# Row sums of the second attention's exponentials: VectorE or GpSimd

## The chip, the cores and the metric

The kernel runs on one core of a Trainium2 chip. The metric is the device time of one execution in microseconds (us), and the median of several runs is compared. A core has five engines with queues of their own: TensorE (PE, with its weight loads shown as PEld), VectorE (DVE), ScalarE (ACT), GpSimd (POOL) and SyncE (SP), which issues most transfers. Each engine takes its instructions in the order of its queue and waits for the others by semaphores. SBUF is the working memory with 128 partitions; PSUM has eight banks of 128x512 f32, into which TensorE writes.

## The reference

One decoder layer on 8 sequences of 100 tokens of width 1024, with a context of 722 tokens for each sequence:

```
x = layernorm(x + retention_attention(x))           # first attention, 8 heads
x = layernorm(x + attention(x, context))            # second attention
x = layernorm(x + (silu(x Wg) * (x Wu)) Wd)         # feed-forward, 4096 hidden
```

The second attention has 16 query heads of 128 that share 4 key/value heads. Its keys are the 722 context tokens followed by the 100 own tokens (causal among themselves):

```
scores = q . k_full * scale + mask       # 100 x 822 for a head
probs  = softmax(scores)                 # exp(scores - max) / sum of exp
out    = (probs . v_full) wo
```

Everything is computed to f32 accuracy.

## The kernel before

All matrix products are made from halves: a value is split into a rounded high part and a low part (`split` and `split2`, line 68: ScalarE casts the high part, VectorE subtracts it from the value to get the low part), and `mm3` (lines 90, 93 and 94) issues three matmuls for each product.

The second attention loops over the 8 sequences `b` and, in each, over the 4 key/value heads `kv`: 32 steps, called heads below. A head holds the 4 query heads that share its keys, so that a row of scores has 4 x 100 = 400 columns, and the 822 keys lie on the partitions, in seven blocks of up to 128. They are worked in the order 6, 5, 0, 1, 2, 3, 4 (`ORDER`); block 6 is small, 54 keys by 216 columns. One head does this:

- `context_keys` and `context_values` project the context (split into the `big` tiles, once for each sequence, by `load_context`) into keys and values. The squares of the keys are summed over the partitions by a GpSimd all-reduce (L706, tile `kss`); the sums go out as a row and come back as a column (L710 and L801), and lines 803 to 810 make the factors `rk` from them. A small GpSimd memset (L700) sets the tail of `kss` after the earlier row has left.
- For each block, TensorE makes the scores in a PSUM bank `s` (4 banks); ScalarE (L830) or VectorE (L826, with the mask) puts them into block `j` of the tile `s` in SBUF, and VectorE keeps the running maximum `mx` (L831, L834). GpSimd's all-reduce over the partitions (L141) gives the maximum `mb` of each column.
- In four steps of 1, 2, 2 and 2 blocks, VectorE subtracts the maximum (L841, L845), ScalarE takes the exponential (L847) and casts the high part `ph`, VectorE makes the low part `pl` (both L68), and VectorE adds the blocks into `sm` (L850; L853 for the small block).
- A second GpSimd all-reduce (L141) adds `sm` over the partitions into `sb`. TensorE multiplies the exponentials with the values into the only PSUM bank `v`.
- Lines 864 to 869 take the reciprocal of `sb` and scale the product; the result is split (`oh`) and sent out (L872).

The tile `s` in SBUF has one buffer: the next head's first scores may be written only when the exponentials of this one have been read. The key tiles `kall` have two. A planner in the compiler's front end sets the order of the instructions on every engine from its own cost estimates and the program's order (`schedule_with_timeline_sim=True`), so that the work of neighbouring heads is interleaved. In the last heads the output projection of the first half of the tokens (`out_proj`) fills TensorE.

Of the kernel before, what the change touches and what calls it, by code (L numbers as in the profile page):

```python
# [11 lines left out]
ALU = mybir.AluOpType  # L12
# [15 lines left out]
R6 = SC + T - 6 * P  # L28
T6 = T - R6
N6 = 4 * R6  # L30
# [10 lines left out]
def decoder_layer(ctx, tc, xT, cT, w1, wo1, w2, wo2, wc, w3, wd, gw, qw, kw, trig, dec, mask, out):  # L41
    nc = tc.nc
# [17 lines left out]
    def bt(ap):  # L60
        return ap.rearrange("p (b t) -> p b t", b=NB)
# [5 lines left out]
    def split2(hi, lo, src):  # L67
        return nc.scalar.copy(hi, src), nc.vector.tensor_tensor(lo, src, f32(hi), ALU.subtract)  # L68
# [70 lines left out]
    def all_red(pool, x, tag, op=RED.add):  # L139
        y = pool.tile([P, N], F32, tag=tag, name=tag)  # L140
        nc.gpsimd.partition_all_reduce(y, x, P, op)  # L141
        return y
# [623 lines left out]
    with sbuf("cx", 2) as p, sbuf("c1", 1) as p1:  # L766

        s = p1.tile([P, NC, N], F32, tag="s", name="s")
# [5 lines left out]
        for b in range(B):  # L774
            if b > 0:
                load_context(b)
            for kv in range(NKV):
# [34 lines left out]
                if b + kv > 0:  # L812
                    s = p1.tile([P, NC, N], F32, tag="s", name="s")
                mx = p.tile([P, N], F32, tag="mx", name="mx")
                def part(ap, c):
                    ap = bt(ap)
                    return ap[0:R6, :, T6:] if c == 6 else ap
# [19 lines left out]
                sm = p.tile([P, N], F32, tag="mx", name="sm")  # L837
                for j0, j1 in ((0, 1), (1, 3), (3, 5), (5, 7)):
                    if j0 == 0:
                        e = s[0:R6, 0, :N6]  # L840
                        nc.vector.tensor_tensor(bt(e), bt(e), part(mb, 6), ALU.subtract)  # L841
                        hl = ph[0:R6, 0, :N6], pl[0:R6, 0, :N6]
                    else:
                        e = s[:, j0:j1]
                        nc.vector.tensor_tensor(e, e, mb[:, None, :].to_broadcast([P, j1 - j0, N]), ALU.subtract)  # L845
                        hl = ph[:, j0:j1], pl[:, j0:j1]
                    nc.scalar.activation(e, e, AF.Exp)  # L847
                    split2(*hl, e)
                    for j in range(max(j0, 2), j1):
                        nc.vector.tensor_tensor(sm, s[:, 1] if j == 2 else sm, s[:, j], ALU.add)  # L850
                    if j0 == 1:
                        s6 = part(sm, 6)
                        nc.vector.tensor_tensor(s6, s6, bt(s[0:R6, 0, :N6]), ALU.add)  # L853
                sb = all_red(p, sm, "mb")
                ov = bank("v")[:, :N]
                for j in (1, 0, 2, 3, 4, 5, 6):
# [413 lines left out]
```

## Time and profile before

| what | value |
|---|---|
| median of 3 runs | 2486.41 us (2483.72 to 2486.9) |
| span of the profiled execution | 2480.1 us; its own total is not given beside the span |
| second attention in the span | 830 to 1610 us |
| busy there: PE, DVE, ACT, POOL | 776.0, 705.3, 469.8, 298.8 us of 780 |
| granted TensorE clock | 1.00 there, 0.999 over the span |
| mean of an addition, L850 and L853 | 0.63 and 0.37 us, on DVE |
| all-reduce of the maxima, of the sums | 1.60 and 2.60 us, on POOL |

The profile is that of one execution. Its span runs from the first to the last instruction; the time of a run holds what lies around the span as well. A group of instructions is listed by line, engine, operation and tiles, then the count, the busy time, the mean of one in nanoseconds, and the time its engine was idle just before, with what ended that idle time. A wait `A <- B` tells that A's engine stood idle until B was done. Windows give each engine's busy time in a stretch of the span. A line with `x2` or `x3` in the timeline merges neighbours of the same kind. `L68` is the helper for all splits, so its groups are told apart by their tiles.

### The profile page before, as it was taken

How to read it: one execution, taken by the hardware profiler on the slowest of the kernel's cores; microseconds unless marked ns; L12 is line 12 of the kernel's file. 1: busy time of each engine (PE TensorE's matmuls, PEld its weight loads, DVE VectorE, ACT ScalarE, POOL GpSimd, SP SyncE). 2: the span in 40 equal slices, each digit the busy share in tenths (PEclk: the TensorE clock that was granted, in tenths of full speed). 3: DMA queues.
4: the chain of work that ended last, by engine and by line, in shares of the span. 5: the costliest groups of instructions: out<-in, count | busy, mean ns of one | idle time of the engine just before them, and what ended most of it. 6: DMA issues, size and time to landing. Idle time of an engine off the chain costs nothing.

```text
span 2480.1 us, 37239 instructions
## 1 busy us (share of the span) xinstructions
PE 2456.9 (99%) x14068; PEld 2436.3 (98%) x14068; DVE 1950.7 (79%) x3101; ACT 1341.0 (54%) x2258; POOL 481.8 (19%) x266
## 2 busy tenths in 40 slices
PE   9999999999999999999999999999999999999997
PEld 9999999999999999999999999999999999999997
DVE  7777877556898798998998999757987777666756
ACT  6667676334888565665566666524544454432221
POOL 0111111100566343443443443100000000000000
PEclk9999999999999999999999999999999999999999
DMA  7333345775544555455455454465455444389731
GB/s 244 112 112 129 132 142 186 242 257 182 173 163 144 196 185 175 130 180 165 154 181 156 155 187 170 156 241 172 160 176 189 161 161 161 122 303 325 265 103 54
DMA packets 221891, 433.98 MB, mean 175 GB/s; under 512 B 47338, under 2 KB 163946, under 8 KB 209294
## 3 DMA queue, kind: packets, MB, share of 16 engines
q1 hardware_dynamic: 217358, 419.49, 50.2%
q0 software_dynamic: 3200, 10.75, 1.9%
q8 instruction: 111, 1.82, 0.3%
q10 hardware_dynamic: 1152, 1.34, 0.2%
q14 instruction: 70, 0.57, 0.1%
HBM read 322.18 MB, written 109.35 MB: 174 GB/s over the span
## 4 chain that ended last, share of the span: by engine, by line
PE 94%; DVE 2%; DMA 2%; ACT 1%; issue 1%; SPq 0%; DVEq 0%; ACTq 0%
PE a L94 20%; PE a L93 20%; PE a L90 20%; PE s L94 9%; PE s L93 9%; PE s L90 9%; PE v L93 2%; PE v L94 2%; PE v L90 2%; PE s L554 1%; PE s L795 1%; PE s L166 1%; DVE y L331 0%; PE v L546 0%; DMA wst<-in_w 0%
## 5 line engine op out<-in xcount | busy, mean ns | idle before, releaser
L90 PE MATMUL a<-big,w 128*128 128x400 f32 (+2 forms) x1808 | 610.7, 339 | 2.0 <-DVE z L270 0.7
L93 PE MATMUL a<-big,w 128*128 128x400 f32 (+2 forms) x1808 | 610.0, 337 | 0.5 <-DVE big L68 0.5
L94 PE MATMUL a<-big,w 128*128 128x400 f32 (+2 forms) x1808 | 608.5, 337 | 0.5 <-DVE w L68 0.5
L68 ACT CAST w<-wst 128x1024 fp32r<-128x1024 f32 (+1 forms) x231 | 239.5, 1039 | 380.3 <-PE s L94 147.6
L68 DVE TENSOR_TENSOR w<-wst,w 128x1024 fp32r<-128x1024 f32 (+1 forms) x231 | 281.1, 1217 | 132.5 <-ACT w L68 130.6
L90 PEld LDWEIGHTS a<-big,w 128*128 128x128 f32 x1808 | 340.2, 188 | 4.5 <-ACT big L68 1.1
L93 PEld LDWEIGHTS a<-big,w 128*128 128x128 f32 x1808 | 340.9, 189 | 2.5 <-DVE big L68 1.3
L94 PEld LDWEIGHTS a<-big,w 128*128 128x128 f32 x1808 | 340.8, 189 | 1.4 <-DVE w L68 0.8
L90 PE MATMUL a<-z,w 128*128 128x400 f32 x680 | 235.0, 346 | 0.4 <-ACT w L68 0.4
L93 PE MATMUL a<-z,w 128*128 128x400 f32 x680 | 235.1, 346 | 0.0
L94 PE MATMUL a<-z,w 128*128 128x400 f32 x680 | 234.9, 346 | 0.0
L90 PE MATMUL s<-big,w 128*128 128x400 f32 x664 | 230.3, 347 | 0.5 <-DMA big<-o2d 0.4
L94 PE MATMUL s<-big,w 128*128 128x400 f32 x664 | 229.2, 346 | 0.4 <-DVE w L68 0.4
L93 PE MATMUL s<-big,w 128*128 128x400 f32 x664 | 229.5, 346 | 0.0
L706 POOL PARTITION_ALL_REDUCE kss<-ksq x64 | 170.2, 2659 | 113.4 <-ACT ksq L705 112.6
L141 POOL PARTITION_ALL_REDUCE ss<-sq x56 | 148.4, 2651 | 199.3 <-ACT sq L750 110.1
L830 ACT ACTIVATE s<-s,rk 128x400 f32<-128x400 f32 x160 | 88.1, 591 | 90.9 <-DVE sm L850 65.3
L90 PEld LDWEIGHTS a<-z,w 128*128 128x128 f32 x680 | 127.8, 188 | 1.2 <-ACT w L68 0.8
L94 PEld LDWEIGHTS a<-z,w 128*128 128x128 f32 x680 | 128.7, 189 | 0.0
L93 PEld LDWEIGHTS a<-z,w 128*128 128x128 f32 x680 | 127.8, 188 | 0.4
L90 PEld LDWEIGHTS s<-big,w 128*128 128x128 f32 x664 | 124.8, 188 | 2.1 <-issue 0.7
L94 PEld LDWEIGHTS s<-big,w 128*128 128x128 f32 x664 | 125.4, 189 | 0.7 <-DVE w L68 0.7
(366 smaller groups left out, 5462.3 us busy)
## 6 DMA issues: line engine op xcount, KB each, us to landing
wst<-in_w SPq DMA_DIRECT2D x135, 512.0 KB
w<-wcd SPq DMA_DIRECT2D x64, 1024.0 KB
wst<-in_wo SPq DMA_DIRECT2D x64, 512.0 KB
hd<-h SPq DMA_DIRECT2D x12, 1400.0 KB
wst<-in_wd SPq DMA_DIRECT2D x64, 256.0 KB
big<-o1d SPq DMA_DIRECT2D x16, 800.0 KB
qd<-d SPq DMA_DIRECT2D x32, 400.0 KB
q<-qd SPq DMA_DIRECT2D x32, 400.0 KB
```

What stands on the lines that cost most here:

```text
L68: return nc.scalar.copy(hi, src), nc.vector.tensor_tensor(lo, src, f32(hi), ALU.subtract)
L90: i = nc.tensor.matmul(acc, lh, rh, start=start, stop=False, skip_group_check=chain)
L93: nc.tensor.matmul(acc, lh, rl, start=False, stop=False, skip_group_check=chain)
L94: nc.tensor.matmul(acc, ll, rh, start=False, stop=stop, skip_group_check=chain)
L141: nc.gpsimd.partition_all_reduce(y, x, P, op)
L166: nc.tensor.transpose(tr[0:T, b * P:(b + 1) * P], vt[:, b * T:(b + 1) * T], ident)
L554: nc.tensor.matmul(bt(o)[:, b], vv[:, b * P:(b + 1) * P], pf[:, b], start=True, stop=True)
L706: nc.gpsimd.partition_all_reduce(ss[:, at], sq[:, at], P, RED.add)
L795: nc.tensor.transpose(tr[0:rows, (c - c0) * P:(c - c0 + 1) * P], vt[:, c * P:c * P + rows], ident)
L830: nc.scalar.activation(sc, sp, AF.Copy, scale=rk[:, c:c + 1])
```

## The change

The additions of lines 850 and 853 are issued on GpSimd instead of VectorE. Tiles, order in the program, and all other instructions stay as they are.

```
                     for j in range(max(j0, 2), j1):
-                        nc.vector.tensor_tensor(sm, s[:, 1] if j == 2 else sm, s[:, j], ALU.add)
+                        nc.gpsimd.tensor_tensor(sm, s[:, 1] if j == 2 else sm, s[:, j], ALU.add)
                     if j0 == 1:
                         s6 = part(sm, 6)
-                        nc.vector.tensor_tensor(s6, s6, bt(s[0:R6, 0, :N6]), ALU.add)
+                        nc.gpsimd.tensor_tensor(s6, s6, bt(s[0:R6, 0, :N6]), ALU.add)
```

## The prediction

> **What bounds the kernel now.** I began with the page's busy table and its chain, to see which engine sets the end; then the busy time in stretches, with the second attention (830 to 1610 us) cut into 100 us pieces; then TensorE's own waits in it.
>
> ```profile
> PE 2456.9 (99%) x14068; PEld 2436.3 (98%) x14068; DVE 1950.7 (79%) x3101; ACT 1341.0 (54%) x2258; POOL 481.8 (19%) x266
> PE 94%; DVE 2%; DMA 2%; ACT 1%; issue 1%; SPq 0%; DVEq 0%; ACTq 0%
> ```
>
> ```profile
> 930.00:1030.00 100.00, 100.00 (x608) 99.36 (x607) 90.37 (x156) 60.11 (x117) 40.49 (x21) 1.00 0.49 156
> ...
> 1700.00:2000.00 300.00, 298.47 (x1629) 296.58 (x1628) 245.42 (x355) 151.03 (x223) 0.00 (x0) 1.00 0.46 161
> ```
>
> ```profile
> PE v L93 <- DVE pl L68: 1.8, 2, 1.6
> PE s L90 <- DVE vall L68: 1.5, 1, 1.5
> PE a L90 <- DVE z L270: 0.7, 1, 0.7
> ```
>
> In the stretches the columns after the length are PE, PEld, DVE, ACT, POOL, then granted clock and DMA. All six 100 us pieces from 930 to 1530 show PE at 100.00 and clock 1.00; 830 to 930 has 98.47, 1530 to 1610 (80 us) has 77.52. PE is therefore idle 1.53 + 2.48 = 4.0 us in the whole stage, and the waits add to the same 4.0. A busy PE could hide stalls inside its modelled ends, but its pace says no: in the feed-forward layer, 300 us hold 1,629 matmuls, 0.184 us each, nearly all 400 columns wide; the attention's 608 in 100 us (0.164 us each) mix 400 columns with 360, 216 and 128.
>
> VectorE is the second engine: the eight pieces sum to 705.3 us of 780. The all-reduces of the sums run from 853.16 to 1596.67 us, 31 periods, so a head takes 24.0 us; over 32 heads VectorE has 22.0 us busy and 2.3 us idle each. POOL has 298.8 us in the stage, 9.3 a head.
>
> **The change part by part.**
>
> ```profile
> L850 DVE TENSOR_TENSOR sm<-sm,s 128x400 f32<-128x400 f32 x128 | 80.8, 631 | 0.8
> L850 DVE TENSOR_TENSOR sm<-s 128x400 f32<-128x400 f32 x32 | 19.2, 600 | 0.0
> L853 DVE TENSOR_TENSOR sm<-sm,s 54x216 f32<-54x216 f32 x32 | 11.8, 368 | 0.0
> L141 POOL PARTITION_ALL_REDUCE mb<-mx x32 | 51.0, 1595 | 90.4 <-DVE mx L831 90.4
> L141 POOL PARTITION_ALL_REDUCE mb<-sm x32 | 83.3, 2602 | 208.9 <-DVE sm L850 208.9
> L700 POOL MEMSET kss<- 128x46 f32 x29 | 4.0, 137 | 63.8 <-DMA row<-kss 63.8
> L773 POOL MEMSET vall<- 128x256 f32 x2 | 0.6, 311 | 8.5 <-DMA kd<-d 8.5
> ```
>
> These groups of the stage show, after the bar, busy us, mean ns of one, and the idle time before.
>
> *Removed from VectorE:* 160 + 32 additions, 80.8 + 19.2 + 11.8 = 111.8 us, 3.5 us a head. Off the path, because PE does not wait for VectorE from 930 to 1530. Of the 4.0 us of PE idle, only the 1.8 us for the lows of the exponentials (`pl`), in the last heads, sit behind these additions; I credit 1.0.
>
> *Added to POOL:* five 128x400 additions and one 54x216. No POOL addition is in this trace. Bounds: VectorE's 0.56 us below, the adding all-reduce's 2.60 above. The two memsets give 174 ns for 210 more columns, 0.83 ns a column and pass, so 0.43 us for writing 400. An addition has two reads and a write: 0.76 us if a read runs beside the write, 1.1 if nothing overlaps. I take 1.0 us, nearest to the memsets, and 0.6 for the small one: 5.6 us a head. With VectorE's 0.56 and 0.37 it is 3.2, with the all-reduce's 2.60 (and 216/400 of it) 14.4. POOL then has 9.3 + 5.6 = 14.9 us of 24.0 (12.5 to 23.7), not a bound by amount.
>
> A rule speaks against the change. The Trainium skill, "GPSIMD Engine Reference", section 4.1 (Engine selection), wants elementwise work on VectorE and calls GpSimd about twice as slow; its table for 2048 columns has 4497 against 2293 ns. By it, an estimate from that page, an addition costs 1.96 x 0.56 = 1.1 us and a head about 6.2 us, without a single PE wait more, as POOL would have 15.5 of 24.0 us. No run here shows it yet.
>
> *The engines meet.* POOL's and VectorE's instructions hold each other up when both read pairs from SBUF. A head's two timelines show it:
>
> ```profile
> 1276.90 2.46 POOL L706 PARTITION_ALL_REDUCE kss<-ksq  x1
> 1285.43 3.07 POOL L706 PARTITION_ALL_REDUCE kss<-ksq  x1 [4.63 <-ACT ksq L705]
> 1289.39 2.60 POOL L141 PARTITION_ALL_REDUCE mb<-sm  x1 [0.89 <-DVE sm L850]
> ```
>
> ```profile
> 1277.03 1.74 DVE L841 TENSOR_TENSOR s<-s,mb 54x216 f32<-54x216 f32 x1 [0.33 <-POOL mb L141]
> 1286.12 2.57 DVE L850 TENSOR_TENSOR sm<-sm,s 128x400 f32<-128x400 f32 x2
> 1289.35 0.37 DVE L826 SCALAR_TENSOR_TENSOR s<-s,msk 54x216 f32<-54x216 f32 x1
> ```
>
> L841 took 1.74 us beside an all-reduce; its shortest is 0.36. Summing mean less undisturbed duration over the stage's VectorE groups (L841 16 us, L831 19, the `oh` split 11, L850 9, L834 7, the context splits 6, L866 5, L809 5) gives about 79 us, 2.5 a head, against 9.3 of POOL work: 27% of POOL's time is lost on VectorE. By that share the additions cost VectorE 5.6 x 0.27 = 1.5 us a head; if all of it collides, 5.6. They run while VectorE makes the lows from pairs in SBUF, so I take 60%, 3.4. Net of the 3.5 removed: -0.1 (between -2.0 and +2.1), below its 2.3 us of idle. Cost on PE nothing; if that cover went, each us past it would cost 32 us in all. The Trainium skill, "SBUF — State Buffer", section "Who interferes with whom", has the loser blocked for the whole instruction; L841's 1.74 us agrees in kind. Taken literally for every addition it is the 5.6 us case.
>
> *The new order.* The additions now stand in POOL's queue behind the memset of `kss`, which waits for a row transfer (63.8 us in 29 times), and ahead of or behind the next key norm's all-reduce (L706) and the sums' own (L141). Who waits: that all-reduce, then L864 to L872; the row transfer and the factors `rk`, if L706 stands behind; and, since the tile `s` has one buffer, the next head's first evictions (L826 on VectorE, L830 on ScalarE, with the key and value evictions queued behind). ScalarE already waits there: 65.3 us in 24 times for L850. In the head shown the last exponential ended at 1283.0 and the sum at 1289.3, 6.3 us later, as VectorE had the lows to make. POOL could begin near 1281.0 and needs 5.6, so 1286.6; if the key all-reduce goes first (2.5), 1289.1. Level, so nothing. In the head before, exponentials ended at 1255.7, the sum at 1263.3, and POOL stood idle from 1253.0 to 1263.3: there it is earlier. The later sum all-reduce has cover: its `v` bank is read (L869) at 1296.68 us while the next products into it come after the next exponentials, which start at 1299.41.
>
> Every DMA stays on its queue; POOL's own transfer issues in the stage are five, at its end (L264, after the last sum). SP issues nothing new. The planner reorders the engines' work by its own costs; I price that at 0, with 3 us to either side. Sum: -1.0 (removed) + 0 (additions on POOL) + 0 (meeting) + 0 (order) = -1.0. The profiled span is 2480.1 us, so 2479.1; the page gives no total for that execution beyond the span, and the median of the three runs lies 6.3 above it (3.6 to 6.8): 2485.4.
>
> **The rivals.**
>
> *The sum comes late (slower).* Place: L826 and L830 waiting on POOL. For: one buffer of `s`, and ScalarE's 65.3 us. Against: POOL's 6.5 us of idle before each sum all-reduce (208.9/32). Price: 1281.0 + 5.6 + 3.3 (POOL held by the four lows) + 2.5 (key all-reduce) = 1292.4, 3.1 later than 1289.3. Heads without context work take 22.0 us between their L841 (1277.03 to 1299.01), against 24.0 on average: 2.0 us of slack. It decides above that: 1.1 us x 32 = 35 us, 2521; in one head of four, 9 us, 2495.
>
> *VectorE becomes the bound (slower).* It decides when it loses more than 3.5 + 2.3 = 5.8 us a head, just past the 5.6 of full collision. With additions of 1.3 us (7.2 a head) and all colliding, 1.4 x 32 = 45 us, 2531; at 14.4 us a head, (14.4 - 5.8) x 32 = 275 us, 2761, which needs both far ends. Against: the measured share is 27%.
>
> *The freed VectorE clears PE's idle (faster).* At most all 4.0 us of the stage, 2482; that is under 0.2%, so a real gain needs the planner to shorten another stage too, where PE idles 3.0 us before 600 and 16.1 after 1610.
>
> **How the numbers follow.** About 0.2%, 5 us, is what a measurement of this kernel can tell from no change. Forecast 0.55 (own range 2481 to 2490); late sum 0.22; VectorE bound 0.17; a gain past 5 us 0.06. So faster 0.06, same 0.55, slower 0.39. The low end is the full clearing and 2 us of the order's 3, 2480; the high end 2518 reaches into both slow rivals and leaves some 0.14 above and 0.03 below.
>
> **What the changed profile would show.** Right: L850 and L853 on POOL near 1.0 and 0.6 us; VectorE near 705 us in the stage, POOL near 480; PE still at 100.00 per 100 us; the period of the sum all-reduces still 24.0. Late sum: ScalarE's wait L830 <- POOL `sm` well above 65 us, and PE waiting at `s` or `a`. VectorE bound: its busy share above 97%, `pl` and L845 lengthened, PE waiting for `pl`. I am wrong if the additions take much over 1.3 us, or if the planner's new order puts PE's score products where they wait for `s`.

## The result and the profile after

The changed kernel takes 2865.18 us in the median (2859.82 to 2868.61) against 2485.43 us (2483.72 to 2486.9): 1.1524 times as long, 95% interval 1.1508 to 1.154. The forecast was no change.

The page of the changed kernel: the busy table, rows of the 40 slices, and the chain by engine.

```profile
PE 2571.2 (90%) x14068; PEld 2524.6 (88%) x14068; DVE 1876.3 (65%) x2909; ACT 1329.3 (46%) x2258; POOL 690.9 (24%) x458
PE   9999999999996677777878877777999999999998
POOL 0001001016643344444444444442000000000000
PEclk9999999999997888888898898888999999999999
PE 57%; POOL 13%; issue 11%; DVE 8%; DMA 5%; ACT 5%; SPq 0%; POOLq 0%; DVEq 0%; ACTq 0%
```

TensorE is no longer busy all through the second attention; elsewhere it is as before. GpSimd and "issue" (time in which an engine waited for nothing that the profile shows) are now a quarter of the chain. In stretches, with the same columns as before:

```profile
930.00:1030.00 100.00, 69.33 (x380) 67.11 (x378) 45.15 (x76) 32.69 (x65) 39.39 (x27) 0.86 0.28 87
1330.00:1430.00 100.00, 76.74 (x408) 74.17 (x407) 56.47 (x94) 42.78 (x83) 44.40 (x32) 0.89 0.38 120
```

VectorE fell from 90 us in a hundred to 45 to 56, so it has not become the bound. Where the time is, the groups on GpSimd in the stage tell; the last columns are the idle time before them and what ended it:

```profile
L850 POOL TENSOR_TENSOR sm<-sm,s 128x400 f32<-128x400 f32 x128 | 133.3, 1041 | 23.0 <-issue 15.2
L141 POOL PARTITION_ALL_REDUCE mb<-sm x32 | 83.8, 2618 | 192.9 <-issue 192.9
L141 POOL PARTITION_ALL_REDUCE mb<-mx x32 | 51.7, 1615 | 92.1 <-DVE mx L831 92.1
L850 POOL TENSOR_TENSOR sm<-s 128x400 f32<-128x400 f32 x32 | 39.3, 1227 | 236.0 <-issue 73.5 <-ACT big L68 35.9 <-DVE rk L810 27.7
L853 POOL TENSOR_TENSOR sm<-sm,s 54x216 f32<-54x216 f32 x32 | 21.4, 668 | 2.5
```

The additions cost what was forecast (1.04 us, the first of each head 1.23, and 0.67 for the small one). But GpSimd stands idle 236.0 us ahead of the 32 first additions, 7.4 us each, and 192.9 us ahead of the 32 all-reduces of the sums, 6.0 us each, with nothing to wait for. The view puts part of the 236.0 us down to the last events of other engines (`big`, `rk` and more), but an addition reads none of these tiles, and its gap is between 6.65 and 9.13 us whatever name stands there. The all-reduce waits for the last addition, its own engine's instruction just before it. The timeline of GpSimd for one head:

```profile
1284.12 2.62 POOL L141 PARTITION_ALL_REDUCE mb<-sm  x1 [5.88 <-issue]
1291.54 1.72 POOL L141 PARTITION_ALL_REDUCE mb<-mx  x1 [4.80 <-DVE mx L831]
1293.16 2.52 POOL L706 PARTITION_ALL_REDUCE kss<-ksq  x1
1296.35 3.67 POOL L706 PARTITION_ALL_REDUCE kss<-ksq  x1 [0.66 <-ACT ksq L705]
1307.15 1.04 POOL L850 TENSOR_TENSOR sm<-s 128x400 f32<-128x400 f32 x1 [7.13 <-issue]
1308.27 0.61 POOL L853 TENSOR_TENSOR sm<-sm,s 54x216 f32<-54x216 f32 x1
1308.83 0.13 POOL L700 MEMSET kss<- 128x46 f32 x1
1308.96 4.34 POOL L850 TENSOR_TENSOR sm<-sm,s 128x400 f32<-128x400 f32 x4
1319.13 2.62 POOL L141 PARTITION_ALL_REDUCE mb<-sm  x1 [5.83 <-issue]
```

The step from an all-reduce to an addition has a gap of 7.1 us here, the step back one of 5.8, and no other step of the engine in this head has a gap without something to wait for. The blocks that the first two additions read were done before the gap began: the last exponential of this head ended at 1299.75 us on ScalarE, the key all-reduce at 1300.02. What stands in the gaps is in the answer for the line of the additions; the second fence is the line of the all-reduces in the kernel before:

```profile
L850 POOLq MODIFY_POOL_CONFIG  x68: 87/88/98, 852.2 to 1952.2; - x68
```

```profile
L141 POOLq MODIFY_POOL_CONFIG  x2: 330/330/330, 39.0 to 39.0; - x2
```

GpSimd changes its configuration each time: 138 such records under lines 850, 706 and 141, two for each change, so 69 changes, 68 of them in the stage. Before, there was one in the whole kernel, ahead of the first all-reduce. Nearly all of the records last 90 ns or less, and they stand at the start of the gaps: in this head at 1300.0 us, for the gap that ends at 1307.15. What the engine does in the rest of a gap the trace does not show: the DMA queues for instructions carry 182 packets here and 181 before.

The head shown is 1319.13 - 1284.12 = 35.0 us long, and on GpSimd it is 2.6 (sums) + 4.8 (waiting) + 1.7 (maximum) + 2.5 + 0.7 (waiting) + 3.7 (keys) + 7.1 (change) + 6.2 (additions) + 5.8 (change): 29.6 us of it work or change. Over the stage the all-reduces of the sums run from 871.0 to 1974.7 us, 35.6 us a head instead of 24.0. 31 x 11.6 = 360 us is nearly all of the difference between the spans, 2866.5 - 2480.1 = 386 us; the first of these all-reduces is also 18 us later. The other engines meet it in their own queues. ScalarE's timeline in the same head:

```profile
1313.34 1.08 ACT L830 ACTIVATE s<-s,rk 128x400 f32<-128x400 f32 x2 [9.38 <-POOL sm L850]
1321.78 0.54 ACT L864 ACTIVATE r<-mb 128x400 f32<-128x400 f32 x1 [7.36 <-POOL mb L141]
1322.35 0.54 ACT L865 ACTIVATE r<-r 128x400 f32<-128x400 f32 x1
1322.79 1.55 ACT L830 ACTIVATE s<-s,rk 128x400 f32<-128x400 f32 x3
```

Two of the next head's evictions wait for the additions, since `s` has one buffer. The other three stand behind the logarithm (L864), which the planner put between them and which waits for the change back and the all-reduce. TensorE waits for evictions on both engines. Its scores (L90) wait for VectorE's L826, ahead of which VectorE stood idle 211.9 us in the stage for the additions; the transposes of the values (L795), which use the banks `s` too, wait for ScalarE's L830:

```profile
PE s L90 <- DVE s L826: 144.9, 29, 18.9
PE s L795 <- ACT s L830: 97.8, 30, 6.3
```

### The profile page after: what moved, and what is told of

It reads as the page before. It is cut to its first block, busy times and chain, and to the rows that moved or that the text cites. A ratio compares the mean times of both kernels' runs of the same rounds, so it can differ in the third digit from the quotient of the medians.

```text
span 2866.5 us, 37439 instructions
## 1 busy us (share of the span) xinstructions
PE 2571.2 (90%) x14068; PEld 2524.6 (88%) x14068; DVE 1876.3 (65%) x2909; ACT 1329.3 (46%) x2258; POOL 690.9 (24%) x458
## 4 chain that ended last, share of the span: by engine, by line
PE 57%; POOL 13%; issue 11%; DVE 8%; DMA 5%; ACT 5%; SPq 0%; POOLq 0%; DVEq 0%; ACTq 0%
PE a L94 12%; PE a L93 12%; PE a L90 12%; PE s L94 6%; PE s L93 6%; PE s L90 6%; POOL sm L850 6%; POOL mb L141 4%; POOL kss L706 2%; DMA rr<-row 1%; DVE s L841 1%; DVE pl L68 1%; PE s L554 1%; ACT ph L68 1%; DVE mx L831 1%
## 5 line engine op out<-in xcount | busy, mean ns | idle before, releaser
L90 PE MATMUL a<-big,w 128*128 128x400 f32 (+2 forms) x1808 | 628.0, 348 | 17.0 <-DVE z L270 13.6
L93 PE MATMUL a<-big,w 128*128 128x400 f32 (+2 forms) x1808 | 626.2, 347 | 0.3 <-DVE big L68 0.3
L94 PE MATMUL a<-big,w 128*128 128x400 f32 (+2 forms) x1808 | 623.5, 346 | 0.7 <-DVE w L68 0.7
L90 PEld LDWEIGHTS a<-big,w 128*128 128x128 f32 x1808 | 354.4, 196 | 20.0 <-DVE z L270 13.9
L93 PEld LDWEIGHTS a<-big,w 128*128 128x128 f32 x1808 | 355.2, 196 | 2.3 <-DVE big L68 1.4
L94 PEld LDWEIGHTS a<-big,w 128*128 128x128 f32 x1808 | 354.7, 196 | 2.5 <-DVE w L68 1.0
L90 PE MATMUL s<-q,kall 128*128 128x400 f32 (+1 forms) x224 | 99.9, 446 | 156.5 <-DVE s L826 144.9
L90 PE MATMUL a<-z,w 128*128 128x400 f32 x680 | 234.7, 345 | 0.4 <-ACT w L68 0.4
L90 PE MATMUL s<-big,w 128*128 128x400 f32 x664 | 230.7, 348 | 1.5 <-DMA big<-o2d 1.2
L706 POOL PARTITION_ALL_REDUCE kss<-ksq x64 | 186.7, 2918 | 95.8 <-ACT ksq L705 84.0
L830 ACT ACTIVATE s<-s,rk 128x400 f32<-128x400 f32 x160 | 84.5, 588 | 255.3 <-POOL sm L850 245.6
L90 PEld LDWEIGHTS s<-q,kall 128*128 128x128 f32 (+1 forms) x224 | 53.2, 238 | 169.2 <-DVE s L826 153.6
L866 DVE TENSOR_TENSOR mb<-mb,r 128x400 f32<-128x400 f32 x32 | 18.4, 575 | 213.7 <-ACT r L865 213.7
L826 DVE SCALAR_TENSOR_TENSOR s<-s,msk 54x216 f32<-54x216 f32 x32 | 12.0, 374 | 211.9 <-POOL sm L850 211.9
L68 DVE TENSOR_TENSOR pl<-s,ph 128x800 fp32r<-128x800 f32 (+1 forms) x128 | 127.8, 1018 | 28.1 <-ACT ph L68 26.8
```

The lines of the kernel that those rows point to most:

```text
L90: i = nc.tensor.matmul(acc, lh, rh, start=start, stop=False, skip_group_check=chain)
L93: nc.tensor.matmul(acc, lh, rl, start=False, stop=False, skip_group_check=chain)
L94: nc.tensor.matmul(acc, ll, rh, start=False, stop=stop, skip_group_check=chain)
L706: nc.gpsimd.partition_all_reduce(ss[:, at], sq[:, at], P, RED.add)
L830: nc.scalar.activation(sc, sp, AF.Copy, scale=rk[:, c:c + 1])
L866: nc.vector.tensor_tensor(sb, sb, r, ALU.mult)
```

## The experiments

Four theories. A: GpSimd needs one library for additions and another for the all-reduce (library is the name used here for what the configuration records exchange), each change costs 6 to 7 us, and these make the loss. B: the additions do it, by their own length on GpSimd or by holding VectorE up at SBUF. C: any further instruction between two all-reduces costs this. D, on how the changes reach TensorE: not through the evictions' waits, but because GpSimd's queue sets the pace. The kernels ran on more than one chip; each ratio is against the kernel before on the same chip, where its median lay between 2484.6 and 2486.3 us. A head's length is taken from the first and the last all-reduce of the sums.

### One addition instead of six

```
-  nc.vector.tensor_tensor(sm, ...)
+  (nc.gpsimd if j == NC - 1 else nc.vector).tensor_tensor(sm, ...)
```

> Only the last of the six additions (block 4, 128x400) is on GpSimd, the other five stay on VectorE. Theory A, GpSimd changes its instruction library between an all-reduce and an addition and back: two changes a head remain (64 in the stage), the one behind the addition (about 5.9 us) is in the chain of the sums in full, the one ahead may be hidden behind VectorE's additions. A head 28 to 32 us long instead of 24.0: 2610 to 2750 us. Theory B, the additions themselves are slow on GpSimd or hold VectorE up: a fifth of the additions' time is left, so about a fifth of the 380 us: 2550 us or less.

Measured: 2830.34 us, 1.1399 times the kernel before (1.1382 to 1.1416), 34.9 us a head. With a sixth of the additions, 346 of the 380 us remain. Theory B falls as the main cause. Theory A had the sign and most of the size, but 2830 lies above its range: it expected that the change ahead of the addition might hide behind VectorE's additions. It can't, by this kernel's GpSimd timeline: the change starts only once the key all-reduce is over, and that one waits 8.81 us for the squares of the keys (L705), which ScalarE makes from TensorE's products.

```profile
1257.35 2.48 POOL L706 PARTITION_ALL_REDUCE kss<-ksq  x1 [8.81 <-ACT ksq L705]
1267.60 1.01 POOL L850 TENSOR_TENSOR sm<-sm,s 128x400 f32<-128x400 f32 x1 [7.77 <-issue]
1274.49 2.62 POOL L141 PARTITION_ALL_REDUCE mb<-sm  x1 [5.88 <-issue]
```

### All additions, no all-reduce beside them

The second attention's all-reduces are left out, in the changed kernel and in the kernel before.

```
-  nc.gpsimd.partition_all_reduce(ss[:, at], sq[:, at], P, RED.add)   # squares go straight to ss
-  mb = all_red(p, mx, "mb", RED.max)
+  mb = mx
-  sb = all_red(p, sm, "mb")
+  sb = sm
```

> All additions on GpSimd as in the changed kernel, but the second attention's all-reduces are left out (each partition's own squares, maxima and sums are used, so the softmax is not the reference's): 192 additions, one library change instead of 68. Theory A: as fast as the same kernel with its additions on VectorE, within 10 us, and TensorE at 99% and more in the stage, 2470 to 2495 us. Theory B: most of the 380 us stays, over 2700.

> The same left out, with the additions on VectorE: the partner of the kernel without all-reduces. Both theories: TensorE is the bound, at or a little under the kernel before, 2470 to 2490 us.

Measured: 2485.81 us with the additions on GpSimd (1.0009, 0.9999 to 1.0018), 2478.67 us with them on VectorE (0.9982, 0.9972 to 0.9991). With all 192 additions on GpSimd and no change of library among them, the loss is 7.1 us, not 380. Those 7 us are what is left for theory B. The two kernels' groups show the lows lengthened while GpSimd reads; that this is the way by which the 7 us reach TensorE is not shown, since its idle time in the stage differs by 2.2 us only.

```profile
L68 DVE TENSOR_TENSOR pl<-s,ph 128x800 fp32r<-128x800 f32 x96 | 133.9, 1407 | 12.7 <-ACT ph L68 12.6
```

```profile
L68 DVE TENSOR_TENSOR pl<-s,ph 128x800 fp32r<-128x800 f32 x96 | 93.9, 979 | 7.6 <-ACT ph L68 7.3
```

The first is with GpSimd's additions, the second without. VectorE's busy time in the stage rose from 639.1 to 656.4 us although 72.2 + 17.9 + 11.8 = 101.9 us of additions had left it: it lost 119 us, 3.7 a head. GpSimd's additions were lengthened as well: 292.5 us in all, 9.1 a head, with means of 1.44 and 1.91 us for the two 128x400 groups and 1.47 for the small one, against 194 us in the changed kernel, whose VectorE was far less busy. The second kernel also shows how little could have been won: without any all-reduce and its waits, 0.18%.

### One idle addition, one idle copy

One GpSimd instruction a head is added to the kernel before, behind the maximum's all-reduce. Its result is read by nobody.

```
   mb = all_red(p, mx, "mb", RED.max)
+  nc.gpsimd.tensor_tensor(junk, mb[0:R6, :N6], mb[0:R6, :N6], ALU.add)   # first kernel
+  nc.gpsimd.tensor_copy(junk, mb[0:R6, :N6])                             # second kernel
```

> The kernel before (all additions on VectorE), plus one small GpSimd addition a head (54x216, about 0.6 us) of the maxima into a tile that nobody reads. Theory A: 64 library changes come with it; GpSimd then has 9.3 + 0.6 + 13 = 23 us of work and changes in a head of 24.0, and its all-reduces come late in some heads: 2520 to 2800 us. Theory B: 0.6 us on an engine with 14 us to spare, nothing depends on it: 2486 us within 5.

> The partner of the kernel with an idle addition a head on GpSimd: the same place, tile and shape (54x216), but a copy instead of an addition. Theory A (library changes cost the time) holds that a copy needs none, since its instruction list shows none beside it: 2485 us within 5, against 2617.5 for the addition. Theory C (any further GpSimd work between two all-reduces costs this): near 2617.

Measured: 2617.52 us with the addition (1.0542, 1.0526 to 1.0558; 28.3 us a head), 2486.36 us with the copy (1.0002, 0.9993 to 1.0012; 24.0). Place, shape and count are the same. The timelines of GpSimd, addition first; the fence behind it is from the answer for the line of the addition, and the copy's line has no such record:

```profile
1275.66 2.46 POOL L706 PARTITION_ALL_REDUCE kss<-ksq  x1
1285.16 0.54 POOL L837 TENSOR_TENSOR junk<-mb 54x216 f32<-54x216 f32 x1 [7.04 <-issue]
1285.65 0.13 POOL L700 MEMSET kss<- 128x46 f32 x1
1292.11 2.62 POOL L141 PARTITION_ALL_REDUCE mb<-sm  x1 [6.33 <-issue]
```

```profile
L837 POOLq MODIFY_POOL_CONFIG  x64: 87/88/88, 843.7 to 1723.6; - x64
```

The timeline with the copy:

```profile
1278.01 2.46 POOL L706 PARTITION_ALL_REDUCE kss<-ksq  x1
1280.35 2.76 POOL L837 COPY junk<-mb 54x216 f32<-54x216 f32 x1
1283.06 0.13 POOL L700 MEMSET kss<- 128x46 f32 x1
1286.53 3.73 POOL L706 PARTITION_ALL_REDUCE kss<-ksq  x1 [3.34 <-ACT ksq L705]
```

Theory C falls, and theory A stands in its cleanest form: the instruction that brings changes with it costs 133 us, the one that doesn't costs nothing that can be told from noise (its interval holds 1), although its record is three times as long in the median (2.77 against 0.85 us). An idle change costs less than one in the sums' path (64 changes each, 133 us here and 346 with the real addition).

A further look has three kinds side by side:

```
+  if kv % 2 == 0: nc.gpsimd.tensor_copy(junk, mj)
+  elif kv == 1:   nc.gpsimd.tensor_scalar(junk, mj, 2.0, None, ALU.mult)
+  else:           nc.gpsimd.tensor_tensor(junk, mj, mj, ALU.add)
```

> The same idle GpSimd instruction a head, but a copy in heads 0 and 2 of each sequence, a multiplication with a constant in head 1, an addition in head 3. Theory A: gaps of 6 to 7 us on GpSimd before and after the multiplication and the addition, none around the copies; half the changes, so 2530 to 2570 us. Theory C: gaps around all of them, near 2617.

Measured: 2523.16 us in one run. Its GpSimd timeline, with the multiplication at L841, the addition at L843 and the copy at L839:

```profile
1236.94 0.64 POOL L843 TENSOR_TENSOR junk<-mb 54x216 f32<-54x216 f32 x1 [6.87 <-issue]
...
1252.76 2.46 POOL L706 PARTITION_ALL_REDUCE kss<-ksq  x1
1255.11 2.75 POOL L839 COPY junk<-mb 54x216 f32<-54x216 f32 x1
...
1284.22 0.83 POOL L841 TENSOR_SCALAR junk<-mb 54x216 f32<-54x216 f32 x1 [7.29 <-issue]
```

A multiplication needs the change as well; a copy behind an all-reduce and the memset do not. Half the changes cost 38 us instead of 133, less than the 45 to 85 expected: at 25.2 us a head, the heads without a change make up for part of it (from the sum of 1243.64 us to the next, with the copy, 20.5 us; from there to the next, with the multiplication, 28.7).

### More changes, the same work

All six additions on GpSimd, reading the rounded highs `ph` instead of `s`. The planner then puts the key all-reduces between the additions.

```
-  nc.gpsimd.tensor_tensor(sm, s[:, 1] if j == 2 else sm, s[:, j], ALU.add)
+  nc.gpsimd.tensor_tensor(sm, f32(ph[:, 1]) if j == 2 else sm, f32(ph[:, j]), ALU.add)
```

> The changed kernel with all six additions on GpSimd reading ph instead of s (the sums leave the low parts out). The planner mixes additions and key all-reduces more: 139 library changes instead of 68, with the same 192 additions and all-reduces. Theory A by dose: 139 x 6.5 us of changes and 480 us of work on GpSimd make 1385 us of a stage that took 780, so GpSimd's queue alone is the bound: 3050 to 3250 us. Theory B (the additions, the tile s): under 2865, since s is freed sooner.

Measured: 3259.3 us in one run, 48.6 us a head, 394 us above the changed kernel and just above theory A's range; B's fell. Its trace has 139 changes in all, the changed kernel's 69: 70 more, 5.6 us for each. The counts of the other instructions are the same, but their order and the tile that the additions read differ, so the figure is a dose and not a clean pair. A stretch of its GpSimd timeline shows five changes within one head:

```profile
1264.40 2.45 POOL L706 PARTITION_ALL_REDUCE kss<-ksq  x1 [7.53 <-ACT s L830]
1274.68 1.01 POOL L850 TENSOR_TENSOR sm<-sm,ph 128x400 f32<-128x400 f32 x1 [7.83 <-issue]
1281.48 2.39 POOL L706 PARTITION_ALL_REDUCE kss<-ksq  x1 [5.79 <-issue]
1291.49 2.15 POOL L850 TENSOR_TENSOR sm<-sm,ph 128x400 f32<-128x400 f32 x2 [7.62 <-issue]
1293.58 0.14 POOL L700 MEMSET kss<- 128x46 f32 x1
1299.69 2.62 POOL L141 PARTITION_ALL_REDUCE mb<-sm  x1 [5.97 <-issue]
```

The 7.53 us is a change too (L706 has two configuration records at 1257.1 us), though the view puts it down to another engine's last event.

### Which wait carries it to TensorE

Two waits were taken away from the kernel with one addition: the evictions behind the logarithm (lines 864 to 872 moved), and the tile `s` (the addition reads `ph`).

```
-  nc.scalar.activation(r, sb, AF.Ln)          # and the lines after it, in their place
+  with tc.issue_after(put.ins), tc.issue_after(top.ins):   # put, top: last L830 and L831
+      late.pop()()                            # the same lines, of the head before
```

> The kernel before with one thing moved: the steps behind the sums' all-reduce (reciprocal, scaling, sending, lines 864 to 872) are placed on their engines behind the next head's last score eviction and maximum. No GpSimd addition. TensorE is the bound and the steps have cover: 2485 us within 6.

> The last addition on GpSimd (2830 us) together with the move of lines 864 to 872 behind the next head's evictions. Theory A in full: of the 10.9 us by which a head was longer, the part in which ScalarE stands at the reciprocal for the change back and the all-reduce, with three evictions behind it, goes; the maximum then waits only for GpSimd's queue, some 5 us sooner: 30 us a head, 2640 to 2720 us. Rival D (the order on ScalarE doesn't matter, GpSimd's own queue sets the pace): 2830 within 20.

> The last addition on GpSimd (2830 us), but it reads the rounded high part ph of its block instead of the tile s, so that the sum of that block leaves the low part out and the tile s is free once VectorE and ScalarE are through with it. Theory A with the tile s as the way: the evictions of the next head no longer wait for the change ahead of the addition; what is left is ScalarE standing at the reciprocal and GpSimd's own queue (about 24 us of work and changes a head): 27 to 31 us a head, 2580 to 2720 us. Rival D (GpSimd's queue alone sets the pace): within 20 of 2830.

> Both: the last addition reads ph, and lines 864 to 872 stand behind the next head's evictions (2777 us with the second alone). The block's low part is left out of the sum here too. Theory A: no eviction waits for a library change in either place; GpSimd has 7.3 + 1.0 + 5.9 + 2.6 + 1.6 + 2 x 2.5 = 23.4 us a head in its own queue, and 24.0 is TensorE's: 24 to 28 us a head, 2490 to 2620 us. Rival D: near 2777.

| kernel | us | against before | a head, us |
|---|---|---|---|
| before, lines moved | 2502.43 | 1.0069 (1.0054 to 1.0084) | 24.5 |
| one addition | 2830.34 | 1.1399 (1.1382 to 1.1416) | 34.9 |
| one addition, lines moved | 2777.43 | 1.1171 (1.1152 to 1.119) | 33.2 |
| one addition, reads `ph` | 2805.70 | 1.1289 (1.1269 to 1.1309) | 34.1 |
| both | 2790.47 | 1.1225 (1.1208 to 1.1243) | 33.7 |

The move alone costs 17 us, against the expected nothing; why is open. The three others moved little: 53, 25 and 40 us of 346. None lies in the range that theory A had given, and only the last (2790 near 2777) lies where D had put it. Each wait was there, but with it taken away the head stayed nearly as long. In the kernel with both, no eviction waits for a change, and its waits read:

```profile
ACT r L869 <- POOL mb L141: 327.0, 32, 15.5
DVE mb L871 <- ACT r L870: 244.5, 24, 15.8
POOL kss L706 <- ACT ksq L705: 230.7, 45, 10.0
```

```profile
PE s L796 <- DVE cvt L719: 114.6, 16, 11.6
PE s L796 <- ACT cvt L719: 95.5, 11, 10.6
```

The first fence is of all engines, the second of TensorE. ScalarE and VectorE stand at the reciprocal (L869, L871), 10.2 us at a time on average and 13 us in a head looked at, with the value copies (L719) behind it. TensorE's transposes wait for these copies, so its next key products are late. GpSimd waits for the keys' squares, and only then, behind the keys' all-reduces, does the change begin. So the two changes seem to stand in series with TensorE whichever wait is removed. The strong form of D, GpSimd being full, is wrong too: in this kernel it works or changes only 24.2 us of a head looked at (33.65 from sum to sum, less 9.47 of waiting for the keys). That these waits close a circle is read from the waits and the timeline; no kernel opened all of them at once.

## Why the prediction was wrong

- *TensorE bounds the stage and the gain is at most 4.0 us.* Right in the main: the kernel without all-reduces, which drops the all-reduces' waits besides, gained 5.9 us.
- *Added to POOL: 1.0 and 0.6 us, 5.6 a head, 14.9 of 24.0 us in all.* The durations were right in the changed kernel (1.04 and 0.67 for most; 194 us, 6.1 a head), in part by luck: with TensorE and VectorE at their old pace, in the kernel without all-reduces, they were 1.44 to 1.91 us, over the 1.3 that the prediction named as a sign of being wrong. The sum was wrong, and this is the step that failed: it took GpSimd's time to be the sum of its instructions. An addition beside an all-reduce has two changes, 7.4 + 6.0 = 13.4 us a head, more than twice the additions and nearly as much as the 14.9 us that had been counted. GpSimd then has 29.6 us (the head shown) where a head took 24.0; that alone is 5.6 of the 11.6 us, and the rest is waiting. The trace of before had the sign of it, two MODIFY_POOL_CONFIG records ahead of the first all-reduce, and I did not ask what they were for. Its bounds, made from memsets and all-reduces, could not show it: the memset is one of the instructions that need no change.
- The Trainium skill has the price, on the page that the prediction cites for another: "GPSIMD Engine Reference", section 2.1 (Instruction dispatch), says that this engine's kernels can be loaded at run time and that the first call after a load pays about 6 us with no visible instruction. In the changed kernel the gaps average 6.0 us on the way back to the all-reduce, which agrees, and 7.4 us ahead of the additions, which is longer. That code is loaded in the gaps is the page's account: the traces show the configuration records, the gaps and what brings them. The prediction weighed another rule, that of twice VectorE's time, and its 1.1 us for an addition was close to the 1.04 measured; the time lost lay outside the additions.
- *The engines meet: 3.4 us a head lost on VectorE, net about 0.* Near, partly by luck: 3.7 us in the pair without all-reduces, but as 41% of 9.1 us of additions and not 60% of 5.6; the whole time of that pair differs by 7 us. A block for the whole instruction, which the section cited there states for VectorE's two-port modes and which the prediction took as its worst case, did not show in the lines it printed: L841 ended at 1278.77 us, 0.59 us before the all-reduce beside it.
- *The new order: level, so nothing.* Wrong in consequence. The sum was put at 1289.1 at the latest, level with before; each change alone made it 6 to 7 us later. The rival of the late sum named the place (L826 and L830 waiting for GpSimd, 211.9 and 245.6 us in the stage) but was priced at 1.1 us a head where 11.6 were lost. Its cap, additions and one key all-reduce in the way, left out the changes. Its signs are the ones that came: ScalarE's wait for `sm` at 245.6 us instead of 65.3, and TensorE waiting at `s`.
- *VectorE becomes the bound.* Did not happen: 45 to 56 us busy in the hundreds shown.
- The sum, -1.0 us, missed +380; of the 386 us between the spans, 360 are the longer heads. Its 1.0 us of gain was tested by no run alone.

## What to carry to other kernels

GpSimd's time is not the sum of its instructions: look at which of them need a library, and count how often the queue goes from one to the other. An elementwise addition or multiplication beside a partition all-reduce costs about 7 us of GpSimd's time ahead of it and about 6 behind it here, for one addition or six in a row alike; a copy or a memset costs none. An idle gap put down to "issue" on GpSimd, with a MODIFY_POOL_CONFIG record in it, is the sign.

When a queue gains such a wait, taking one or two other waits out from behind it may win little (25 to 53 us of 346 here), if other instructions of the same loop stand behind it as well.

## What was not expected of the hardware

- The granted TensorE clock was lower where TensorE waited: 1.00 in the stage before, 0.83 to 0.89 in the 100 us stretches of the changed kernel, 0.947 over its span. TensorE's busy time for the same 14,068 matmuls rose with it, from 2456.9 to 2571.2 us; so by the profile, which models the ends of matmuls, 114 of the 386 us are longer matmuls and 272 more idle time. How much shorter a head would be with the changes at the full clock was not measured.
- The change is not short in proportion to the work: one 0.54 us addition stands between 13.4 us of gaps (7.04 and 6.33).
- A GpSimd copy of 54x216 elements has a median record of 2.77 us between the all-reduces (0.36 at its shortest), where the addition of that shape took 0.85 in the median (0.53 at its shortest); why is open, and it cost nothing there. The profile's spans on this engine are rough.
